# A GPS graph layer on one core: the last edges go into the table beside the first sort, and ScalarE makes the first 0/1 matrices

## The chip, the core and the metric

The kernel runs on one core of a Trainium2 chip. The time is that of one execution on the device, in microseconds (us). The engines are named as in the profile: PE is TensorE (PEld is its loading of weights), DVE is VectorE, ACT is ScalarE, POOL is GpSimd and SP is SyncE, which here issues DMA transfers. A transfer whose addresses come from a list of indices (a gather, or a scatter that adds) is issued by POOL.

## The reference, cut to what matters

One layer of a graph network over N = 6250 nodes with D = 256 features and E = 200 000 edges. Edge e goes from node `dst[e]` (whose row is read) to node `src[e]` (to which it is added). `src` is uniformly random. `dst` is skewed to low numbers, and the edges come sorted by `dst`.

```python
xn  = layernorm(x)
# 1. gated mean over edges
neigh = xn[dst]
w     = sigmoid(relu(neigh @ W1 + b1) @ W2 + b2)         # one gate an edge
num   = segment_sum(neigh * w, src, N); den = segment_sum(w, src, N)
gnn   = where(den > 0, num / max(den, 1e-12), 0)
# 2. a linear attention of 8 heads of 32 over all nodes
k, v  = head_ln(xn, klw, klb), head_ln(xn, vlw, vlb)     # d / (std + eps), std of n - 1
mix   = xn_heads @ (k^T v / N) + xn
x     = x + gnn + mix
# 3. six experts of three layers, the two best of each node mixed
f     = layernorm(x)
p     = softmax(relu(f @ rw1 + rb1) @ rw2 + rb2); top 2, softmax over these
out   = x + sum_top2 gate_e * (relu(relu(f @ ew1 + eb1) @ ew2 + eb2) @ ew3 + eb3)
```

The gate depends on the neighbour alone, so `w` and `neigh * w` are one row a node, and the edge part is a sum of such rows into segments. All is computed from the inputs on the chip, the order of the edges by `src` too.

## The kernel before

**The edges.** For each node the kernel makes a row of 258 numbers (neigh * w, w, 1), split into three bf16 terms whose sum carries the float32 value, and stores it in `y_rows`. The edges are cut by position. The first 65 536 (piece b, "hot") have neighbours in the first six node tiles of 128 and are handled by counting matrices, without gathers. The next 65 536 (piece a) and 65 536 (piece c) are "cold": their rows are gathered. The last 3392 are the "few", 27 tiles of at most 128.

**The sorts.** A cold piece is sorted by `src` with a bitonic network on DVE, 128 partitions by 512. Steps along a row are pairs of min and max (`first` and `step`, L263, L278, L279). When partitions have to be compared, `turned` (L308, L309) transposes the whole tile with four PE transposes and one ACT copy for each 512 columns, and back later. The first sort orders piece a alone. The second (`sort cb`) orders c and b side by side, 1024 wide, in 307 DVE instructions and 14 turns; its tiles are `k_cb` and `t_cb`. The sorted keys go to `list_a`, `list_c` and `list_b` in memory. Where each node tile's edges start in a list comes from `counts` (L361): one ACT `Sign` over the 128x512 sources with a sum, for each of the 48 borders between tiles, for a and for c; and 24 of them for b.

**The cold passes** (class `Cold`, L840 to L913). A pass takes a block of two node tiles (256 nodes). SP reads the start (a value load) and loads a window of 12 x 128 list entries for each tile and piece (`cold_load`, L790, L791). `decode` transposes the window on PE (L815), copies it on ACT (L817), and takes the two indices apart on DVE (`dsts` L824, `srcs` L826, `loc` L865). A step then handles 128 edges: POOL gathers 128 rows of `y_rows` (L877, tile `gt`), DVE makes a 128x128 0/1 matrix that says which edge goes to which node (L885, tile `hot`), and PE multiplies the matrix with the three terms (L902, tile `pu`). `make` runs ten steps ahead of the matmuls (AHEAD), with 20 buffers of `gt` and 16 of `hot`. The passes are six blocks of a (144 steps), the same six blocks of c (144), then the other blocks with both pieces (888): 1176 steps. When the first window of c is to be loaded, the rest of the second sort is written out first (`piece_sorted`). `decode` of the next pass is called at the 12th step of a pass.

**The few edges.** `few_equals` (L488 to L505) finds on DVE which of 128 edges share a target and to which row of `table` each writes. `few_edges` gathers 128 rows (L516, POOL), adds up those of one target with three matmuls (L532), copies the sums on ACT (L536, tile `sm`) and adds them into `table` with a scatter from POOL (L537). All scatters write the same table, so each waits for the one before to land. `table` is set to zero by SP beforehand (L445), and is read in the main part.

**The other work of the front.** `deviations` (L459 on) and two lines of `node_rows` (L551 to L606) make the normalized nodes and `y_rows`. `head_squares` (L659 to L686) and `heads` (L702 to L742) make the 32x32 head matrices. `expert_loads` (L959) loads the experts' weights through SP; the router's weights are loaded from ACT's queue (L943).

**The order.** The queues of PE, DVE, ACT, POOL and SP are written out in advance by a planner. Each of the jobs above is a `Line`, a generator that yields after each piece of work how many nanoseconds of DVE time it took and how long its next piece should wait. `run(lines, until)` takes the first line in the list that is due and whose `before` lines are closed, and moves a planned clock on. The first stage runs sort a, the nodes and the counts of a to their end. Then the cold steps of a start, and in the loop

```python
        while line_c.open:
            cold_edges.step()
            clock[0] += 200.0
            due += 2200.0
            run(beside, due)
```

one step alternates with 2200 ns of planned other work, until the few edges are done; a second loop goes on at 1300 ns a step until all jobs of the front are closed. Each engine works through its queue strictly in that order.

**The main part** then goes over the groups of four node tiles: `node_terms` (first matmul L1100), the hot edges by counting (L1047 to L1084), the cold steps of the blocks, and the router and six experts (L1203 to L1267; L1215, L1228 and L1245 are their three layers on PE), with the cold steps placed between the experts' matmuls.

Of the kernel before, what the change touches and what calls it, by code (L numbers as in the profile page):

```python
# [49 lines left out]
def kernel(  # L50
# [229 lines left out]

    def took(n):
        return 2 * (TT0 + 1.05 * n)

    def rows_sorted(k, name, width):

        h = 1
        while h < ROW:
            g = h  # L290
            while g:
                o = sp_small.tile([P, width], FP, name=f"k_{name}", bufs=2)
                if g == h:
                    first(k, o, h, last=2 * h == ROW)
                else:
                    step(k, o, g)
                k, g = o, g // 2
                yield took(width // 2), 0
            h *= 2
        return k  # L300

# [10 lines left out]
    def merged(k, name, width, m):  # L312

        t = turned(k, f"t_{name}", width)
        yield 0, TURN
        g = h = 1 << (m - 1)
        while g:
            o = sp_small.tile([P, width], FP, name=f"t_{name}", bufs=2)
            if g == h:
                first(t, o, h, last=2 * h == P)  # L320
            else:
                step(t, o, g)
            t, g = o, g // 2
            yield took(width // 2), 0
        k = turned(t, f"k_{name}", width)
        yield 0, TURN
        g = ROW // 2
        while g:
            o = sp_small.tile([P, width], FP, name=f"k_{name}", bufs=2)
            step(k, o, g)  # L330
            k, g = o, g // 2
            yield took(width // 2), 0
        return k


    TT0 = 150.0
    TURN = 2300.0


    pad = sp_small.tile([P, max(p.cap for p in pieces)], FP, name="pad")  # L340
# [11 lines left out]
            nc.sync.dma_start(lists[p.name][: p.n].rearrange("(p t) -> p t", p=P), k[:, i * ROW : (i + 1) * ROW])  # L352
            nc.sync.dma_start(lists[p.name][p.n :].rearrange("(p t) -> p t", p=P), pad[:, : p.cap])

    def counts(i):


        p = pieces[i]
        junk = sp_small.tile([P, p.row], BF, name=f"junk_{p.name}")
        for b in range(SB - 1 if p is hot else 0, NTHR, SB if p is hot else 1):  # L360
            nc.scalar.activation(  # L361
                junk, raw[p.name][0], AF.Sign, bias=thr[:, b : b + 1], accum_out=cnts[:, i, b : b + 1]
            )
            yield 0, 60 + 1.1 * p.row

    starts = const.tile([P, len(pieces), NTILE], I32, name="starts")
    nc.vector.memset(starts, 0)
# [140 lines left out]
    def few_edges():  # L508

        got = {}  # L510

        def gather(i):
            if i < NFEW:
                r = min(P, E - FEW - i * P)
                gt = gp.tile([P, TERMS, W], BF, name="gt")
                nc.gpsimd.indirect_dma_start(  # L516
                    out=gt[:r].rearrange("p k w -> p (k w)"),
                    out_offset=None,
                    in_=y_rows,
                    in_offset=bass.IndirectOffsetOnAxis(ap=few[1][:r, i : i + 1], axis=0),  # L520
                )
                got[i] = r, gt

        gather(0)
        gather(1)
        for i in range(NFEW):
            gather(i + 2)
            yield 0, 4500
            r, gt = got.pop(i)
            ps = p_t.tile([P, GT * P], FP, name="pT")  # L530
            for k in range(TERMS):
                nc.tensor.matmul(  # L532
                    ps[:r, :W], few_eq[:r, i, :r], gt[:r, k], start=(k == 0), stop=(k == TERMS - 1)
                )
            sm = nw.tile([P, W], FP, name="sm", bufs=3)
            nc.scalar.copy(sm[:r], ps[:r, :W])  # L536
            nc.gpsimd.indirect_dma_start(  # L537
                out=table,
                out_offset=bass.IndirectOffsetOnAxis(ap=few_row[:r, i : i + 1], axis=0),
                in_=sm[:r],  # L540
                in_offset=None,
                compute_op=ALU.add,
            )
# [76 lines left out]
    def run(lines, until=None):  # L620
# [16 lines left out]
        if until is not None:  # L637
            clock[0] = max(clock[0], until)


    worst = const.tile([P, 3], FP, name="worst")
    most = const.tile([P, 1], I32, name="most")
# [47 lines left out]
    def heads():  # L690
# [3 lines left out]
        for g, t0, nt, rows, r in groups:  # L694
            while g not in hsqs:
                yield 0, 1000
            xt, hsq = xts.pop(g), hsqs.pop(g)
            for j0 in range(0, nt, 2):
                k = min(2, nt - j0)
                for j in range(k):  # L700
                    for c in range(CB):
                        nc.tensor.matmul(  # L702
                            dv[:r, (j * CB + c) * P : (j * CB + c + 1) * P], xt[:, j0 + j, c, :r], centre,
                            start=True, stop=True,
                        )
                yield 0, 1800
                z = zs[j0 // 2]
                nc.vector.tensor_tensor(
                    z[:r, : k * CB, :P].rearrange("p b (h c) -> p b h c", c=HC),
                    dv[:r, : k * CB * P].rearrange("p (b h c) -> p b h c", h=HB4, c=HC),  # L710
                    hsq[:r, j0 * CB : (j0 + k) * CB, :, None].to_broadcast(
                        [r, k * CB, HB4, HC]
                    ),
                    op=ALU.mult,
                )
                for j in range(k):
                    for c in range(CB):
                        zc = z[:r, j * CB + c, :]
                        t = t0 + j0 + j
                        nc.tensor.matmul(  # L720
                            kv_ps[c][:, : P + 1], zc[:, :P], zc, start=(t == 0), stop=(t == NTILE - 1)
                        )
                yield 700, 0
# [38 lines left out]
    line_d = Line(deviations())  # L762
    lines_y = [Line(node_rows(i), before=[line_d]) for i in range(2)]
    line_t = Line(few_equals())
    line_c = Line(few_edges())
    line_u = [Line(counts(i)) for i in range(3)]
    line_a, line_b = Line(sort(pieces[:1])), Line(sort(pieces[1:]))
    line_q = Line(head_squares(), before=lines_y + [line_a])
    line_h = Line(heads(), before=lines_y + [line_t, line_a])
    line_l = Line(other_loads())  # L770
    line_e = Line(equal_keys(), before=[line_u[2], line_b, line_h])
    with tc.manual_schedule(engines=ORDERED):
        clock[0] = 6000.0
        line_d.due = 12000.0
        line_l.due = 16000.0
        line_u[1].before = line_u[2].before = lines_y
        line_t.before = [line_l]
        line_u[0].due = 9000.0
        first_lines = [line_u[0], line_l, line_d] + lines_y + [line_a, line_t]
        while any(a.open for a in first_lines):  # L780
            run(first_lines + [line_q, line_h, line_u[1], line_u[2], line_b], clock[0] + 1000.0)
        starts_of(0)


# [32 lines left out]
        nc.scalar.copy(keys.bitcast(FP), pT[:, :n])  # L817
        return keys, n

    def cold_window(wt):  # L820

        keys, n = window_keys(wt, "a")
        dsts = wn.tile([P, SB * NCOLD], I32, name="dsts")[:, :n]
        nc.vector.tensor_scalar(dsts, keys, (1 << LOW) - 1, None, op0=ALU.bitwise_and)  # L824
        srcs = wn.tile([P, SB * NCOLD], I32, name="srcs")[:, :n]
# [9 lines left out]
    for i, (blk, ps) in enumerate(passes):  # L835
        first_step.append(len(steps_c))
        for half in range(min(SB, NTILE - blk * SB)):
            n = sum(p.cap for p in ps)
            todo = range(half * n, (half + 1) * n)
            steps_c += [(i, half, j, j == todo[0], j == todo[-1]) for j in todo]  # L840

    class Cold:


        def __init__(self, sorted_to):
            self.made, self.done, self.loaded, self.sorted_to = 0, 0, 0, sorted_to
            self.wt, self.keys, self.gts, self.hot = {}, {}, {}, {}
            self.sums, self.parts = {}, {}
            self.load(0)
            self.load(1)  # L850
# [1 line left out]
        def load(self, i):  # L852

            while self.loaded <= min(i, len(passes) - 1):
# [3 lines left out]
                self.wt[self.loaded] = cold_load(blk, ps)  # L858
                self.loaded += 1

        def decode(self, i):
            self.load(i)
            dsts, srcs = cold_window(self.wt.pop(i))
            loc = wn.tile([P, SB * NCOLD], FP, name="loc")[:, : srcs.shape[1]]
            nc.vector.tensor_scalar(loc, srcs, float(-passes[i][0] * BN), None, op0=ALU.add)  # L865
            self.keys[i] = dsts, loc

        def make(self):
            i, half, j, _, _ = steps_c[self.made]
            at = self.made - first_step[i]  # L870
            if at == 2 and i + 1 < len(passes):
                self.load(i + 1)
            if at == 12 and i + 1 < len(passes):
                self.decode(i + 1)
            dsts, loc = self.keys[i]
            gt = gp.tile([P, TERMS, W], BF, name="gt")
# [5 lines left out]
            )  # L882
            self.gts[self.made] = gt
            hot1 = hp1.tile([P, P], BF, name="hot1")
            nc.vector.tensor_scalar(  # L885
                hot1, count[:, half * P : (half + 1) * P], loc[:, j : j + 1], None, op0=ALU.is_equal
            )
            self.hot[self.made] = hot1
            self.made += 1

# [34 lines left out]
    known = [cold[0]]  # L925
    with tc.manual_schedule(engines=ORDERED):
        cold_edges = Cold(lambda p: p is cold[0] or piece_sorted(p))
        beside = [line_c, line_u[1], line_q, line_h, line_u[2], line_b, line_e]
        run(beside[1:], clock[0] + 9000.0)
        cold_edges.decode(0)  # L930
        run(beside[1:], clock[0] + 2000.0)
        due = clock[0]
        while line_c.open:
            cold_edges.step()
            clock[0] += 200.0
            due += 2200.0
            run(beside, due)
    n_work.__exit__(None, None, None)

# [43 lines left out]


    line_w = Line(expert_loads())
    beside = [line_w, line_u[1], line_q, line_h, line_u[2], line_b, line_e]
    with tc.manual_schedule(engines=ORDERED):
        load(0)
        while any(a.open for a in beside):
            cold_edges.step()  # L990
            clock[0] += 200.0
            due += 1300.0
            run(beside, due)
        piece_sorted(cold[1])
    h_work.__exit__(None, None, None)
# [500 lines left out]
```

## Time and profile before

| | |
|---|---|
| time, median of 6 runs | 2354.19 us (2344.83 to 2363.0) |
| the profiled execution | 2363.96 us, of which the span of the trace is 2362.0 |
| mean granted TensorE clock over the span | 0.878 |
| PE busy | 1830.8 us (78%), 9541 matmuls; weight loads 1192.0 (50%) |
| DVE busy | 1259.3 us (53%), 5000 instructions |
| POOL busy | 1212.6 us (51%), 1243 instructions |
| ACT busy | 574.0 us (24%), 1199 instructions |

Durations below are those of the one profiled execution. "Issue" as the end of an idle time means that the engine waited for nothing that the profile shows; a name behind an arrow is the work that ended the wait. A weight load (PEld) runs beside the matmuls. A row of the view by stretches gives the stretch and its length, the busy time of PE, PEld, DVE, ACT and POOL with the number of instructions in brackets, the mean granted clock, the share of time that the 16 DMA engines were busy, and GB/s. In the groups a row has the line, engine and operation, the tiles written and read, the number, then the busy time and the mean of one in ns, then the idle time ahead of them and what ended most of it. A row of the waits has who waited for whom, the sum, the number and the longest, in us. In the chain, a row has the time, the length, and the work.

### The profile page before, as it was taken

What the parts mean: (1) busy time and instruction counts of PE and PEld (TensorE: products, weight loads), DVE (VectorE), ACT (ScalarE), POOL (GpSimd) and SP (SyncE); (2) the same over time, 40 slices, a digit from 0 to 9 for tenths busy, and PEclk for the clock granted to TensorE, in tenths of its full rate; (3) what the DMA queues carried; (4) which work ended last, traced back from release to release, by engine and by line L of the source; (5) the groups of instructions that cost most, each with busy time, mean ns of one, the idle gap of its engine ahead of it and who ended that gap; (6) DMA issues with size and microseconds to landing.
All of it is one profiled execution on the core that took longest, in us unless ns stands there. A gap on an engine that the chain in (4) does not pass through costs nothing.

```text
span 2362.0 us, 30158 instructions
## 1 busy us (share of the span) xinstructions
PE 1830.8 (78%) x9541; PEld 1192.0 (50%) x9541; DVE 1259.3 (53%) x5000; ACT 574.0 (24%) x1199; POOL 1212.6 (51%) x1243
## 2 busy tenths in 40 slices
PE   1571598543366898999889898998989889899997
PEld 0341377332243555655556555565655556556555
DVE  8699675664256553545435454454455535554321
ACT  6772542100001211212111121211212112122332
POOL 0000487874656566666666666566666656661000
PEclk9675599666687898999999999999999989999999
DMA  8650366564544455455555555555555555451000
GB/s 240 186 194 16 104 169 141 136 206 129 155 123 132 141 141 167 134 141 165 142 163 141 144 153 136 157 142 148 151 141 164 143 160 139 135 162 49 15 9 13
DMA packets 163584, 320.54 MB, mean 136 GB/s; under 512 B 31353, under 2 KB 104298, under 8 KB 163418
## 3 DMA queue, kind: packets, MB, share of 16 engines
q0 software_dynamic: 80800, 241.85, 37.9%
q1 hardware_dynamic: 77262, 76.15, 10.4%
q10 hardware_dynamic: 5356, 0.55, 0.3%
q8 instruction: 77, 1.26, 0.2%
q14 instruction: 89, 0.73, 0.1%
HBM read 285.06 MB, written 33.39 MB: 135 GB/s over the span
## 4 chain that ended last, share of the span: by engine, by line
PE 64%; DVE 6%; another core or an unknown queue 5%; issue 5%; DMA 2%; ACT 1%; POOL 1%; SPq 0%; DVEq 0%; POOLq 0%; ACTq 0%
PE px L1228 22%; PE pu L902 16%; PE px L1245 10%; PE ph L1075 5%; PE ph L1056 4%; PE px L1215 2%; PE ph L1100 1%; DMA gt<-y_rows,dsts 1%; DVE fr L1049 1%; PE px L1135 1%; DVE to L1047 1%; DVE hot L885 1%; PE turn L308 1%; DVE k_cb L278 1%
## 5 line engine op out<-in xcount | busy, mean ns | idle before, releaser
L877 POOL DMA_INDIRECT gt<-y_rows,dsts x1176 | 1132.8, 963 | 910.9 <-DVE srcs L826 263.7
L902 PE MATMUL pu<-gt,hot 128*128 128x258 bf16 x3528 | 604.1, 288 | 43.9 <-DMA gt<-y_rows,dsts 17.5
L902 PEld LDWEIGHTS <-hot 128*128 128x128 bf16 x3528 | 357.0, 103 | 415.8 <-issue 330.9
L1237 ACT ACTIVATE h<-px,eb_t 128x512 f32<-128x512 f32 (+1 forms) x312 | 206.3, 663 | 494.8 <-PE px L1228 203.1
L1228 PE MATMUL px<-fT,ew_t 128*128 128x512 f32 (+1 forms) x624 | 314.2, 599 | 1.6 <-issue 1.6
L1245 PE MATMUL px<-ew_t,h 128*128 128x256 f32 (+1 forms) x1176 | 303.2, 385 | 6.6 <-issue 5.3
L1228 PE MATMUL px<-h,ew_t 128*128 128x512 f32 (+1 forms) x624 | 300.6, 577 | 0.3 <-ACT fT L1129 0.2
L885 DVE TENSOR_SCALAR hot<-count,loc 128x128 bf16<-128x128 bf16 x1176 | 272.0, 273 | 31.9 <-remote 18.0
L1049 DVE TENSOR_SCALAR fr<-count,rdl 128x128 bf16<-128x128 bf16 x884 | 228.3, 274 | 108.9 <-PE pu L902 50.3
L1056 PE MATMUL ph<-to,fr 128*128 128x256 bf16 x884 | 189.9, 285 | 114.6 <-issue 59.0
L1254 DVE SCALAR_TENSOR_TENSOR acc<-px,gate,acc 128x256 f32<-128x256 f32 (+1 forms) x294 | 128.6, 478 | 247.3 <-PE px L1245 117.5
L1245 PEld LDWEIGHTS px<-ew_t,h 128*128 128x128 f32 (+1 forms) x1176 | 206.6, 192 | 38.5 <-issue 14.8
L1047 DVE TENSOR_SCALAR to<-count,hloc 128x256 bf16<-128x256 bf16 x612 | 184.6, 304 | 35.6 <-PE ph L1056 24.1
L1056 PEld LDWEIGHTS <-fr 128*128 128x128 bf16 x884 | 87.8, 100 | 147.8 <-issue 62.5
L1075 PE MATMUL ph<-yh,cn 128*128 128x258 bf16 x882 | 136.8, 280 | 31.0 <-issue 18.7
L1058 ACT CAST cn<-ph 128x256 bf16<-128x256 f32 x150 | 54.4, 374 | 355.9 <-PE ph L1056 210.3
L1075 PEld LDWEIGHTS <-cn 128*128 128x128 bf16 x882 | 87.6, 100 | 58.5 <-issue 43.5
L1228 PEld LDWEIGHTS px<-h,ew_t 128*128 128x128 f32 x624 | 97.0, 192 | 36.7 <-issue 31.9
L1228 PEld LDWEIGHTS px<-fT,ew_t 128*128 128x128 f32 x624 | 101.7, 201 | 24.9 <-issue 17.3
L817 ACT COPY keys<-pT 128x25 f32<-128x25 f32 (+2 forms) x56 | 10.5, 187 | 311.9 <-PE pu L902 94.6
L560 PE MATMUL turn<-ident,xs 128*128 128x128 f32 (+1 forms) x98 | 27.8, 407 | 74.5 <-ACT xs L551 68.1
L1103 DVE TENSOR_TENSOR u<-ph,u 128x256 f32<-128x256 f32 (+1 forms) x49 | 20.7, 423 | 108.0 <-PE ph L1100 38.4
(228 smaller groups left out, 1764.4 us busy)
## 6 DMA issues: line engine op xcount, KB each, us to landing
gt<-y_rows,dsts POOLq DMA_INDIRECT x1176
xs<-in_x_dram SPq DMA_DIRECT2D x24, 512.0 KB
y_rows<-ys SPq DMA_DIRECT2D x10, 774.0 KB
table<-zero SPq DMA_DIRECT2D x50, 129.0 KB
tb<-table SPq DMA_DIRECT2D x49, 129.0 KB
xnT_d<-xnT SPq DMA_DIRECT2D x12, 512.0 KB
xt<-xnT_d SPq DMA_DIRECT2D x12, 512.0 KB
u<-in_x_dram SPq DMA_DIRECT2D x12, 512.0 KB
```

The lines of the kernel that those rows point to most:

```text
L877: nc.gpsimd.indirect_dma_start(out=gt.rearrange("p k w -> p (k w)"), out_offset=None, in_=y_rows, in_offset=bass.IndirectOffsetOnAxis(ap=d ...
L885: nc.vector.tensor_scalar(hot1, count[:, half * P : (half + 1) * P], loc[:, j : j + 1], None, op0=ALU.is_equal)
L902: nc.tensor.matmul(self.pu, hot1, gt[:, k], start=(start and k == 0), stop=(stop and k == TERMS - 1))
L1047: nc.vector.tensor_scalar(made[j1], count, loc[:, j1 : j1 + 1], None, op0=ALU.is_equal)
L1049: nc.vector.tensor_scalar(fr, count[:, :P], rdl[:, d1, j1 : j1 + 1], None, op0=ALU.is_equal)
L1056: nc.tensor.matmul(pa, matrices[i], made[j], start=(j == j0), stop=(j == j1 - 1))
L1058: nc.scalar.copy(cn[:, d], pa)
L1075: nc.tensor.matmul(pu[:, :W], cn[:, d, s * P : (s + 1) * P], yh[:, d, k], start=(d == 0 and k == 0), stop=(d == HOT - 1 and k == TERMS - 1),)
L1228: nc.tensor.matmul(ph[:, :rows], w[:, e, c, f * P : (f + 1) * P], ins[:, c, :rows], start=(c == 0), stop=(c == CB - 1),)
L1237: nc.scalar.activation(h[:, f, :rows], ph[:, :rows], AF.Relu, bias=bc)
L1245: nc.tensor.matmul(po[:r, j - j0], h2[:, c, j * P : j * P + r], ew_t[2][:, e, c, :], start=(c == 0), stop=(c == CB - 1),)
L1254: nc.vector.scalar_tensor_tensor(acc[:r, j, :], po[:r, j - j0], gate[:r, j, e : e + 1], acc[:r, j, :], op0=ALU.mult, op1=ALU.add)
```

## The change

1. **The few edges** start as soon as `node_rows`, `few_equals` and the zeroing of the table are closed, in the first stage beside sort a, ahead of all other lines in the list, at 2400 ns of planned wait a tile instead of 4500. The gathers are issued four ahead instead of two, and `sm` has four buffers instead of three. `few_equals` waits for no line now and is first due at 62 us of the planned clock.
2. **The 0/1 matrices of the first six passes** (144 steps; ON_ACT) are made by two ACT instructions, |loc - count| and then relu(1 - that), instead of one DVE comparison. `loc` has its sign turned for it.
3. **Turn and decode apart.** The window of the next pass is transposed and copied at step 8 of a pass (`turn`), and taken apart on DVE at step 13 (`decode`); both were at step 12.
4. **Counts.** 28 of the 48 counts of piece a stay early, and 20 are made when the rows are done. Those of c and b follow after sort a and at the end of the list. The scrap tile `junk` is one name with two buffers.
5. **Head squares** may start when the rows and the counts of a are done, and no longer wait for sort a.
6. **The planner's figures** are set anew: the price of a sort step and of a turn, the planned times per cold step (2200 to 4100, 1300 to 1500) and the order of the lines.

The core of the diff:

```diff
-    def took(n):
-        return 2 * (TT0 + 1.05 * n)
+    def took(n, apart=False):
+        return 4 * (TT0 + 0.52 * n) if apart else 2 * (TT0 + 1.05 * n)
...
-    TT0 = 150.0
-    TURN = 2300.0
+    TT0 = 120.0
+    TURN = 2600.0
...
-    def counts(i):
+    def counts(i, part=slice(None)):
...
-            yield 0, 60 + 1.1 * p.row
+            yield 0, 900
...
-        gather(0)
-        gather(1)
+        for i in range(4):
+            gather(i)
+        yield 0, 2400
         for i in range(NFEW):
-            gather(i + 2)
-            yield 0, 4500
+            gather(i + 4)
+            yield 0, 2400
...
-            sm = nw.tile([P, W], FP, name="sm", bufs=3)
+            sm = nw.tile([P, W], FP, name="sm", bufs=4)
...
-    line_c = Line(few_edges())
-    line_u = [Line(counts(i)) for i in range(3)]
+    line_l = Line(other_loads())
+    line_c = Line(few_edges(), before=lines_y + [line_t, line_l])
+    line_u0 = Line(counts(0, slice(0, EARLY)))
+    line_u = [Line(counts(0, slice(EARLY, None)), before=lines_y)] + [Line(counts(i)) for i in (1, 2)]
...
-    line_q = Line(head_squares(), before=lines_y + [line_a])
+    line_q = Line(head_squares(), before=lines_y + [line_u[0]])
...
-            run(first_lines + [line_q, line_h, line_u[1], line_u[2], line_b], clock[0] + 1000.0)
+            run([line_c] + first_lines + [line_q, line_b], clock[0] + 1000.0)
...
-    def cold_window(wt):
-
-        keys, n = window_keys(wt, "a")
+    def cold_window(keys, n):
+
...
+    ON_ACT = LEAD
+
...
+            if i < ON_ACT:
+                nc.vector.tensor_scalar(loc, srcs, -1.0, first, op0=ALU.mult, op1=ALU.add)
+            else:
+                nc.vector.tensor_scalar(loc, srcs, -first, None, op0=ALU.add)
...
-            if at == 12 and i + 1 < len(passes):
+            if at == 8 and i + 1 < len(passes):
+                self.turn(i + 1)
+            if at == 13 and i + 1 < len(passes):
                 self.decode(i + 1)
...
+            if i < ON_ACT:
+
+                away = hp1.tile([P, P], BF, name="away", bufs=2)
+                nc.scalar.activation(away, count[:, half * P : (half + 1) * P], AF.Abs, bias=loc[:, j : j + 1])
+                nc.scalar.activation(hot1, away, AF.Relu, bias=ones[:, 0:1], scale=-1.0)
+            else:
+                nc.vector.tensor_scalar(
+                    hot1, count[:, half * P : (half + 1) * P], loc[:, j : j + 1], None, op0=ALU.is_equal
+                )
...
-        beside = [line_c, line_u[1], line_q, line_h, line_u[2], line_b, line_e]
-        run(beside[1:], clock[0] + 9000.0)
+        beside = [line_t, line_c, line_u[1], line_q, line_h, line_b, line_u[2], line_e]
+        run(beside, clock[0] + 9000.0)
+        cold_edges.turn(0)
+        run(beside, clock[0] + 3000.0)
         cold_edges.decode(0)
-        run(beside[1:], clock[0] + 2000.0)
+        run(beside, clock[0] + 2000.0)
         due = clock[0]
         while line_c.open:
             cold_edges.step()
-            clock[0] += 200.0
-            due += 2200.0
+            clock[0] += 30.0 if cold_edges.made < first_step[ON_ACT] else 270.0
+            due += 4100.0
             run(beside, due)
```

## The prediction

> **What bounds the kernel now.** I read the time by stage first, from busy times in stretches whose ends I took from the timeline: first gather of the cold edges at 264 us, end of the second sort at 572, first expert matmuls about 780, last gather about 2130.
>
> ```profile
> 0.00:264.00 264.00, 103.65 (x361) 63.14 (x362) 216.50 (x642) 158.74 (x351) 1.62 (x12) 0.70 0.51 150
> 264.00:545.00 281.00, 180.12 (x1146) 143.03 (x1145) 172.63 (x418) 70.36 (x177) 218.97 (x188) 0.76 0.62 159
> 545.00:610.00 65.00, 25.82 (x148) 18.52 (x148) 31.88 (x87) 3.83 (x9) 30.95 (x32) 0.64 0.47 138
> 800.00:2130.00 1330.00, 1193.97 (x6284) 756.84 (x6285) 663.52 (x3075) 259.09 (x498) 844.85 (x890) 0.95 0.53 148
> 2130.00:2362.00 232.00, 214.83 (x910) 136.95 (x909) 77.83 (x296) 65.59 (x122) 7.68 (x9) 0.97 0.07 19
> ```
>
> After the two stretch numbers come PE, PEld, DVE, ACT and POOL. From 800 us on PE is full (90%, then 93%). What can be won in front of that is time in which PE waits. Up to 264 DVE is the full engine (216.5 of 264) and POOL does nothing. From 264 to 545 no engine looks full, so I took POOL's groups there:
>
> ```profile
> L877 POOL DMA_INDIRECT gt<-y_rows,dsts x133 | 141.3, 1063 | 305.3 <-DVE srcs L826 262.0 <-issue 27.9 <-remote 4.8
> L537 POOL DMA_INDIRECT table<-sm,few_row x27 | 49.0, 1816 | 10.3 <-issue 6.1 <-ACT sm L536 2.1 <-ACT sq L672 1.2
> L516 POOL DMA_INDIRECT gt<-y_rows,dst_c x27 | 29.0, 1073 | 8.2 <-issue 4.3 <-PE pu L902 1.8 <-PE pT L532 0.9
> ```
>
> Each of the 187 is followed by 0.3 us that no wait explains ("issue"): 219 + 187 x 0.3 = 275 of 281 us. POOL is full there, and 78 + 54 x 0.3 = 94 us of it is the few edges. Everything else stands in one written order with it, the turns of the second sort (c and b, 1024 wide) too. The chain shows what its end releases:
>
> ```profile
> 569.43 2.79 DMA gt<-y_rows,dsts
> 572.73 3.79 DMA list_c<-pad
> 576.65 0.38 SPq L791
> 577.08 0.49 SPq L790
> 578.02 1.51 DMA wt_a<-list_c
> 579.93 7.62 PE pu L902 x45
> ```
>
> No edge of piece c can be gathered before list_c is stored, and no node's sum is complete before piece c's passes. So **572 us is the gate**: what comes after it (1790 us) is the same work in both kernels and starts 34 us behind it (first L1100 at 606). In the changed program's order 156 steps of cold edges stand ahead of that line, 154 before. I forecast by how far the gate moves. DVE's waits from 264 to 573:
>
> ```profile
> DVE t_cb L263 <- ACT t_cb L309: 36.4, 7, 13.8
> DVE k_cb L278 <- ACT k_cb L309: 11.6, 6, 2.8
> DVE z L708 <- PE dv L702: 10.2, 5, 4.8
> DVE dsts L824 <- ACT junk_b L361: 9.9, 1, 9.9
> DVE hot L885 <- remote: 9.7, 4, 3.3
> ```
>
> Most is DVE waiting for a turn that PE and ACT reach late.
>
> **The change, part by part. First stage.**
> *Counts.* Of 48 counts of piece a on ACT (0.72 + 0.19, spaced 0.85 us) 20 move behind the rows. 19 stand between 41 and 76 us now, about nine of them ahead of the first w, for which DVE waits 10.3 us. Nine times 0.85: -8 us for the rows, and for DVE.
> *Few equals, earlier.* 8 x (0.59 + 0.38 + 0.59) = 12 us of DVE move from 133-215 to the rows' stretch. DVE is 86% busy there and serves the sort in both places: 0. If the rows wait for it, up to 12.
> *Decode of the first pass.* DVE waits 7.1 us for ACT's keys at 263; now the turn is issued earlier and sort steps stand between: -7.
> *More of the second sort ahead.* In the order, 85 of its 307 instructions stand before the first decode, 65 before: 20 x 0.65 = +13 here, and as much less later.
> *Few edges.* 27 gathers, 27 x 3 matmuls, 27 ACT copies (0.375) and 27 scatters move into the first sort; POOL has 1.6 us of work there, so its 94 us are covered. But every scatter waits until the one before has landed in the table, and all engines' later work queues behind. The chain prices it:
>
> ```profile
> 447.73 3.94 DMA table<-sm,few_row
> 451.88 3.21 DMA gt<-y_rows,dsts
> ```
>
> That is 3.94 + 0.3 = 4.2 us a step where scatters follow each other. 22 of them now stand before the first cold gather on POOL. The last rows are stored at 185.6 us now, 8 earlier then; gather, landing, matmul and copy add 6: 184 + 22 x 4.2 = 276. On DVE's side it is 264 - 8 - 7 + 13 + some 7 for turns of sort a that stand behind matmuls waiting on gathers and behind 20 counts = 269. POOL is later: **first cold gather 276, +12**. Bounds: 264 (scatters as close as POOL allows, 1.8 + 1.1 + 0.6 = 3.5) to 290 (5 us each).
>
> **Second stage, 276 us to the gate.** Three engines, each by itself:
> - DVE: 222 sort instructions left, 111 steps x 1.29 = 143; 25 z (17), hsq (7), kv and decodes (7) = 31; 14 turns, of which an undisturbed one takes 3.4 (last t_cb step over at 557.0, k_cb starts 560.4) = 48. Sum 222; with the 31 inside the turns 191. What it loses: 127 matrices (31.6 busy) and their waits (14.7).
> - POOL: 122 gathers up to the flush of the sort x 1.36 + 5 scatters x 2.1 = 177, then 28 of sort alone (16 steps, 2 turns) = 205. The 27 few cost 94 there before.
> - ACT: 122 matrices, each two dependent ACTIVATEs of 128x128. No such row exists. Below it stands w, 128x4, at 0.26, above it the 128x512 rows at 0.66; between them 128x256 at 0.497 (L593). On the line through the first and last of these, 0.38; two make 0.72 with their overlap. 122 x 0.72 = 88, 62 counts x 0.85 = 53, 28 copies 14, squares 12, rest 7 = 174, plus 28 = 202. At the lower row 122 x 0.52: 178; at the upper 122 x 1.33: 276.
>
> The matrices are made ahead, but now a turn's copy queues behind them on ACT, and behind that DVE. The router loads on ACT (L943) still wait for the last scatter; the t_cb copy lost 18.9 us behind them, 0 to 19 again. I take the longest, 222, and add 20 for the three standing in each other's way: 276 + 242 = **518, -54**. Ends: 276 + 191 = 467 and 276 + 276 + 10 = 562.
>
> A rule of the Trainium skill speaks against this part (ScalarE: Activation LUTs, Rules for kernel authors: relu and adds belong on VectorE, not ScalarE). The rows agree on the engine time, 0.275 us for one on DVE against 0.72; taken as the whole price, 88 - 32 = 56 us would be given back and the gate would stand near 572 again. I hold that POOL's order, not DVE's work, kept the gate, and ACT had 70 of 281 us to do.
>
> *Expert weights on SP.* 18 x 256 KB now come before list_c; four came after it. SP had issued list_c by 573.7: 0. Head squares two groups earlier: the 13.6 us wait of L670 for xt goes, inside the 20.
>
> **Main stage.** The turn of a pass's keys stands 4 steps earlier, the decode 1 later. DVE waits at L824 from 842 on in 14 stretches of over 2 us, 93.6 us together, in which PE was busy 72.0: at most 21.6 to win. The lists are loaded about 45 us ahead (1294.4 against 1340.7), so no new wait. I take -8; ends 0 and -21.
>
> **Sum.** -54 - 8 = -62 on the profiled execution (2363.96, span 2362.0 + 2 around it): 2302. The median of the runs shown is 9.8 lower, 2354.19: **2292 us**.
>
> **Rivals.**
> 1. *ACT takes POOL's place.* Matrices at 0.66 an operation; gate near 562, -10, with -4 in the main stage: 2340. For it: ACT's queue is strictly in order. Against: 128x256 already takes only 0.497.
> 2. *The other side: turns stuck in the queue.* If each of the 14 turns costs 11 us (2 of 14 now cost 13.8 and 12.5) because ACT's copy stands behind matrices and PE's behind matmuls waiting on gathers, 276 + 143 + 31 + 154 = 604: +32, 2386. It decides from (572 - 276 - 174) / 14 = 8.7 us a turn. Against: the mean idle at turns is now 51/13 = 3.9 with POOL full.
> 3. *The few edges eat the first stage.* Scatters at 6 us (their spacing now): first gather 316, of which some 20 is made good by the sort going on: gate 545, 2322.
> 4. *All three engines overlap well:* gate about 480 and 15 in the main stage: 2247.
>
> **How the numbers follow.** Forecast 0.52, rival 1 0.13, rival 2 0.13, rival 3 0.12, rival 4 0.10. Half a per cent, 12 us, is about what a measurement of this kernel can tell. Faster: the forecast, rivals 3 and 4, and half of 1 (0.07): 0.81; same, most of the rest of 1: 0.05; slower: rival 2 and what is left of 1: 0.14. The range leaves out rival 2 and part of 4: 2252 (gate -90) to 2345. The forecast's own range is 2265 to 2325.
>
> **What would show it.** Right: list_c issued near 518; POOL between 276 and then near 90% with only 5 scatters; two ACT rows of 0.35 to 0.45 us; scatters 4.2 apart before 276; first kv matmul 30 to 36 us behind list_c; the stretch from there on as long as now within 20 us; L824's waits in it near none. Wrong: a t_cb wait of DVE over 9 us on average; ACT above 90% busy in the second stage; first cold gather after 290; or a main stage longer than now by more than 15 us, for which I see no cause.

## The result and the profile after

The changed kernel takes 2357.74 us (median of 42 runs) against 2351.51 us before (84 runs). The ratio is 1.0024, with a 95% interval of 1.0012 to 1.0035. That is a quarter of a per cent slower, inside the half per cent that I had called no change. I had forecast 2292 us with a range from 2252 to 2345, so the measured time lies outside it. The profiled execution took 2363.35 us, with a span of 2361.6.

Four of the stretches as before, in the changed kernel (stretch and length, then busy time of PE, PEld, DVE, ACT and POOL with the number of instructions, granted clock, DMA share, GB/s):

```profile
0.00:264.00 264.00, 116.32 (x404) 69.67 (x404) 219.65 (x648) 139.31 (x297) 44.85 (x43) 0.68 0.60 167
264.00:545.00 281.00, 167.96 (x1093) 134.74 (x1093) 151.57 (x289) 170.66 (x474) 169.99 (x157) 0.77 0.54 148
800.00:2130.00 1330.00, 1196.73 (x6298) 760.45 (x6297) 665.19 (x3083) 259.29 (x503) 847.43 (x893) 0.95 0.54 149
2130.00:2361.00 231.00, 215.75 (x907) 137.19 (x905) 76.88 (x292) 63.79 (x118) 6.51 (x7) 0.97 0.07 18
```

The work did move as the diff says. POOL is busy for 45 us in the first stretch (1.6 before), and ACT for 171 us in the second (70 before). In the second stretch POOL went down from 219 to 170 us and DVE from 173 to 152. Nobody is full there any more, and yet the stage ends at the same time. The stores of the two sorted lists, in the line on SP's queue (duration min/median/max in ns, first and last start in us), changed kernel:

```profile
L352 SPq DMA_DIRECT2D list_a<-k_a x1: 362/362/362, 259.3 to 259.3; - x1
L352 SPq DMA_DIRECT2D list_c<-k_cb x1: 383/383/383, 572.1 to 572.1; - x1
```

The same two in the kernel before:

```profile
L352 SPq DMA_DIRECT2D list_a<-k_a x1: 363/363/363, 245.9 to 245.9; - x1
L352 SPq DMA_DIRECT2D list_c<-k_cb x1: 362/362/362, 572.3 to 572.3; - x1
```

The first sort ends 13.4 us later, the gate is where it was. The first gather of the cold edges is at 308.4 us, against 264.2 before and 276 forecast. DVE's waits from the end of the first sort to 364 us show what stood still (who waited for whom, sum, number, longest, in us); then PE's from 195 to 364:

```profile
DVE z L711 <- PE dv L705: 36.3, 6, 17.9
DVE hsq L688 <- issue: 18.5, 1, 18.5
```

```profile
PE pT L533 <- DMA gt<-y_rows,dst_c: 42.5, 9, 13.2
PE pu L923 <- DMA gt<-y_rows,dsts: 20.3, 1, 20.3
```

PE waits for the gathers of the few edges, and then 20 us in one piece for the first cold gather. Behind PE's waiting matmuls stands the `dv` that DVE's `z` needs, and behind that `z` the sort. The longest of these waits, in PE's and DVE's rows (start, length, [idle before <- what ended it]; the `dv` between them starts at 315.95):

```profile
311.68 0.80 PE L923 MATMUL pu<-gt,hot 128*128 128x258 bf16 x3 [20.33 <-DMA gt<-y_rows,dsts]
317.04 0.69 DVE L711 TENSOR_TENSOR z<-dv,hsq 128x512 f32<-128x512 f32 x1 [17.89 <-PE dv L705]
```

DVE had spent 65 us on instructions of the second sort by 320 us before, and 55 in the changed kernel; by 400 us 94 and 79. POOL's own record shows the pace, in the same view:

```profile
206.45 1.61 POOL L538 DMA_INDIRECT table<-sm,few_row  x1 [1.70 <-DMA table<-sm,few_row]
208.36 1.17 POOL L516 DMA_INDIRECT gt<-y_rows,dst_c  x1 [0.30 <-issue]
211.13 1.59 POOL L538 DMA_INDIRECT table<-sm,few_row  x1 [1.60 <-ACT sm L537]
213.02 1.02 POOL L516 DMA_INDIRECT gt<-y_rows,dst_c  x1 [0.30 <-issue]
215.69 1.58 POOL L538 DMA_INDIRECT table<-sm,few_row  x1 [1.66 <-issue]
```

A tile of few edges takes 4.6 to 4.7 us where nothing disturbs it, and 4.93 on average (22 scatters from 201.80 to 305.31). The planner reckons with 2.4 here; in the kernel before it had 4.5.

### The profile page after: what moved, and what is told of

The parts are those of the page before. It is cut to its first block, busy times and chain, and to the rows that moved or that the text cites. A ratio compares the mean times of both kernels' runs of the same rounds, so it can differ in the third digit from the quotient of the medians.

```text
span 2361.6 us, 30298 instructions
## 1 busy us (share of the span) xinstructions
PE 1841.1 (78%) x9541; PEld 1194.9 (51%) x9541; DVE 1238.4 (52%) x4856; ACT 668.5 (28%) x1487; POOL 1206.4 (51%) x1243
## 4 chain that ended last, share of the span: by engine, by line
PE 61%; another core or an unknown queue 8%; DVE 7%; ACT 5%; issue 4%; SPq 0%; ACTq 0%; DMA 0%; DVEq 0%
PE px L1251 21%; PE pu L923 15%; PE px L1268 10%; PE ph L1079 4%; PE ph L1098 4%; PE px L1238 2%; DVE to L1070 1%; DVE fr L1072 1%; PE px L1158 1%; DVE k_cb L278 1%; DVE k_cb L279 1%; ACT junk L361 1%; PE ph L1123 1%; ACT hot L904 1%
## 5 line engine op out<-in xcount | busy, mean ns | idle before, releaser
L1251 PE MATMUL px<-fT,ew_t 128*128 128x512 f32 (+1 forms) x624 | 313.4, 599 | 0.0
L1251 PE MATMUL px<-h,ew_t 128*128 128x512 f32 (+1 forms) x624 | 299.1, 574 | 1.5 <-issue 0.8
L906 DVE TENSOR_SCALAR hot<-count,loc 128x128 bf16<-128x128 bf16 x1032 | 239.6, 276 | 38.0 <-PE pu L923 18.5
L516 POOL DMA_INDIRECT gt<-y_rows,dst_c x27 | 30.0, 1113 | 200.2 <-DVE k_a L279 192.3
L1251 PEld LDWEIGHTS px<-fT,ew_t 128*128 128x128 f32 x624 | 101.7, 201 | 24.5 <-issue 16.8
L1251 PEld LDWEIGHTS px<-h,ew_t 128*128 128x128 f32 x624 | 96.9, 192 | 32.6 <-issue 26.8
L1108 DVE TENSOR_TENSOR cs<-ph,cs 128x258 f32<-128x258 f32 x49 | 20.9, 427 | 147.5 <-PE pu L923 75.1
```

What stands on the lines that cost most here:

```text
L906: nc.vector.tensor_scalar(hot1, count[:, half * P : (half + 1) * P], loc[:, j : j + 1], None, op0=ALU.is_equal)
L1251: nc.tensor.matmul(ph[:, :rows], w[:, e, c, f * P : (f + 1) * P], ins[:, c, :rows], start=(c == 0), stop=(c == CB - 1),)
```

## The experiments

My theory after this reading was that the chain of scatters, twice as slow as the planner's figure, holds up the queues of all engines from 195 us on. The rivals were that ACT's matrices hold up the turns of the second sort, that POOL still bounds the second stage, and that this stage has a length of its own.

All kernels in one table. "Ahead" is the number of few-edge scatters that stand before the first cold gather in POOL's order. Times are us from the profiled execution, the ratio is to the kernel before, with its interval. The last four ran on a chip where the kernel before took 2379.2 us instead of some 2355, so for these the ratio is what compares; in proportion, an estimate, 1789.6 us to the end would be 1808 there. Each row of times is one execution, while the ratio is that of the medians.

| kernel | ahead | first cold gather | list_c | between | list_c to end | ratio |
|---|---|---|---|---|---|---|
| before | 0 | 264.2 | 572.3 | 308.1 | 1789.7 | 1 |
| changed | 22 | 308.4 | 572.1 | 263.7 | 1789.5 | 1.0024 (1.0012 to 1.0035) |
| changed, four tables | 22 | 276.4 | 529.4 | 253.0 | none | none |
| changed, 4700 ns | 12 | 270.4 | 529.0 | 258.6 | 1789.6 | 0.9847 (0.9821 to 0.9874) |
| changed, matrices on DVE | 22 | 315.4 | 583.3 | 267.9 | 1795.4 | 1.0097 (1.0067 to 1.0126) |
| before, matrices on ACT | 0 | 266.0 | 572.1 | 306.1 | 1794.1 | 0.9995 (0.9974 to 1.0016) |
| 4700 ns, matrices on DVE | 12 | 273.0 | 539.7 | 266.7 | 1797.9 | 0.9844 (0.9775 to 0.9913) |
| 4700 ns, turn and decode at 12 | 12 | 271.2 | 526.8 | 255.6 | 1798.3 | 0.9844 (0.9781 to 0.9906) |
| before, few edges early, 4700 ns | 14 | 276.5 | 538.7 | 262.2 | 1791.4 | 0.9875 (0.9813 to 0.9937) |
| changed, 7000 ns | 8 | 269.1 | 540.3 | 271.2 | 1811.3 | 0.9995 (0.996 to 1.003) |
| before, few edges early, 2400 ns | 27 | 333.8 | 603.9 | 270.1 | 1823.4 | 1.0134 (1.0086 to 1.0181) |
| changed, 3600 ns | 17 | 288.0 | 539.4 | 251.4 | 1811.2 | 0.9885 (0.9842 to 0.9929) |
| 4700 ns, heads late | 12 | 268.4 | 490.2 | 221.8 | 1852.3 | 0.9853 (0.9806 to 0.99) |
| 4700 ns, few_equals later | 12 | 263.2 | 520.6 | 257.4 | 1813.2 | 0.982 (0.9768 to 0.9871) |

### Scatters to four tables in turn

```diff
+    tables = [table] + [dram.tile([TROWS, W], FP, name=f"table{i}") for i in range(1, 4)]
...
-                out=table,
+                out=tables[i % 4],
```

> The changed kernel, with the 27 scatters of the few edges going in turn to four tables, so that a scatter need not wait for the one ahead of it; the sums of three of the four tables are left out of the result. Theory (the chain of the few edges, 4.63 us a tile in the trace where the planner reckoned with 2.4, holds up the queues of PE, ACT and DVE from 195 to 344 us): a tile then takes what POOL needs, 1.6 + 1.0 + 2 x 0.3 = 3.2 us, the first cold gather comes near 275 instead of 308, list_c is stored near 540 instead of 572, time 30 us or so below the changed kernel, ratio to before 0.985 to 0.992. Rival A (the matrices on ACT hold up the turns of the second sort): list_c within 10 us of 572, ratio 0.998 to 1.005. Rival B (the second stage has a bound of its own, from the first cold gather on): list_c as early as the first gather, near 540, as by the theory; told apart by the stage's own length, which is 264 us now: 264 again by rival B, shorter or longer by the theory as the stalls at 300 to 363 go.

The kernel counts at its end how many edges it has summed, and goes through all edges again in a slow loop if any are missing. With three of the four tables left out of the sum it did so, and its span of 25 742.7 us tells nothing; only the front, up to the stores of the lists, is read here. POOL's record, in the same view as above:

```profile
206.77 1.75 POOL L539 DMA_INDIRECT table<-sm,few_row  x1 [0.31 <-issue]
208.82 1.14 POOL L517 DMA_INDIRECT gt<-y_rows,dst_c  x1 [0.30 <-issue]
210.27 1.58 POOL L539 DMA_INDIRECT table<-sm,few_row  x1 [0.30 <-issue]
```

```profile
L353 SPq DMA_DIRECT2D list_a<-k_a x1: 363/363/363, 249.5 to 249.5; - x1
L353 SPq DMA_DIRECT2D list_c<-k_cb x1: 382/382/382, 529.4 to 529.4; - x1
```

Without the wait for the landing most tiles take 3.2 to 3.5 us. The first cold gather comes 32.0 us earlier and list_c 42.7 us earlier, and the first sort too ends 9.8 us earlier. Nothing else was changed, the ACT matrices least of all, so the wait of a scatter for the landing of the one before is the cause of these 43 us. Rival A is refuted. What is left is close to rival B: 253 us from the first cold gather to list_c, where it was 264.

### The few edges at the pace that they take: 4700 and 3600 and 7000 ns

```diff
-        yield 0, 2400
+        yield 0, 4700
         for i in range(NFEW):
             gather(i + 4)
-            yield 0, 2400
+            yield 0, 4700
```

> The changed kernel, with the planner told 4700 ns for a tile of few edges instead of 2400, which is what a tile took (4.63 us). 12 scatters then stand ahead of the first cold gather instead of 22, and the rest between the cold steps. Theory (queues held up because the chain was reckoned too short): DVE's waits for dv and hsq between 260 and 363 us (58 us now) fall below 20, first cold gather near 265, list_c near 540, ratio to before 0.983 to 0.992. Rival A (ACT's matrices): list_c within 10 us of 572, ratio 0.998 to 1.005. Rival C (POOL is the bound of the second stage, and every scatter put back there costs it): first gather early, but list_c still after 560.

It took 2321.51 us, 0.9847 of the kernel before, and so faster than both kernels, with the planner's two figures alone. The list of piece c:

```profile
L352 SPq DMA_DIRECT2D list_c<-k_cb x1: 383/383/383, 529.0 to 529.0; - x1
```

The waits that answer to those above, DVE's from 248 to 364 us and PE's from 195 to 364:

```profile
DVE z L711 <- PE dv L705: 35.1, 12, 8.9
DVE hsq L688 <- ACT hsq L686: 4.3, 2, 2.6
```

```profile
PE pu L923 <- DMA gt<-y_rows,dsts: 3.3, 1, 3.3
PE pT L533 <- DMA gt<-y_rows,dst_c: 2.5, 1, 2.5
```

PE's waits for gathers, 62.8 us, are 5.8. The gate is where it was in the experiment before (529.4), by another means. Here the wait for the landing is still there, but nothing is queued behind it too early. DVE's waits for `dv` and `hsq` did not fall below 20 as I expected: for `dv` there are twice as many of half the length, with nearly the same sum. So these waits alone do not make up the 43 us of the gate. Up to list_c DVE works 392 us in both kernels, and what falls is its idle time, from 180 to 137 us: by 12 us from 195 us to the end of the first sort (the changed kernel's waits there, 11.6 us, are for turns of that sort), by 18 from there to 364, and by 14 behind that. Rival C is refuted: 15 scatters back beside the cold steps did not bring the gate back.

> The changed kernel with 3600 ns a tile, between 2400 (22 scatters ahead of the first cold gather, 2357.7 us) and 4700 (12, 2321.5). 17 scatters stand ahead. Theory: first cold gather at 202 + 17 x 4.6 = 281 to 286, second stage 253 to 271, list_c 535 to 555, time 2330 to 2345. Rival (a tile costs only when the queues' order is wrong by more than some amount): first gather below 275 and time within 6 us of 2321.5.

Between the two, as the theory has it, is the first gather, at 288.0. It is 2 us later than I expected, and the second stage, 251.4, is shorter than I expected and the shortest with the heads in it; list_c at 539.4 lies where I had it. The ratio, 0.9885, is below that of the changed kernel, and in proportion the time is 2328 us, a little under the 2330 to 2345 that I expected; but its interval overlaps that of 4700 ns, so these two times are not told apart.

> The changed kernel with 7000 ns a tile of few edges: 8 scatters ahead of the first cold gather, 19 beside the cold steps (12 and 15 with 4700, 22 and 5 with 2400). Theory (with 4700 the stalls are gone, and what is left is DVE, with POOL next): first cold gather near 264, list_c 520 to 540, time within 10 us of 2321.5. Rival (still held up by the chain in the first stage at 4700): list_c before 515, time below 2310. Other rival (POOL bounds, each scatter put back costs its 3 us): list_c after 541.

This one missed. The gate is at 540.3, but the time is that of the kernel before. The rival that POOL bounds the stage had put list_c after 541, and the stage, 271.2 us, is the longest of all changed orders: with 19 scatters put back, this rival is not refuted here. 1811.3 us lie between list_c and the end, 21.7 more than with 4700, and 13 to 20 more than in the three other kernels on the same chip (1791.4 to 1798.3). The count of gathers offers a reason: 119 cold gathers had been issued when list_c was stored, against 136 with 4700, 139 in the changed kernel and 142 before. The loop around the few edges lets 4100 planned ns pass for each cold step, the one behind it 1500, and with 7000 ns a tile the first loop lasts longer. 17 gathers at 1.25 us each are 21 us. Of the 21.7 us, 17.6 lie ahead of the first matmul of the experts' first layer (L1251), which starts 233.8 us behind list_c here and 216.2 with 4700. So the trace fits this reason, but no run of its own tests it.

### The matrices, each way

```diff
-    ON_ACT = LEAD
+    ON_ACT = 0
```

> The changed kernel, with the 0/1 matrices of all passes made by DVE again, all else left. Theory (few edges' chain): the 122 matrices put 32 us of work back on DVE, which waits far longer than that in the stage, so list_c within 12 us of 572 and the ratio to before 0.998 to 1.008. Rival A (the matrices on ACT delay the turns and head squares, and with them DVE): list_c before 550, ratio 0.985 to 0.992.

> The kernel before, with only the matrices of the first six passes moved to ACT (two ACT instructions each), no other part of the change. Theory (in the kernel before POOL's order is what bounds 264 to 545): list_c within 10 us of 572, ratio 0.995 to 1.003. Rival A (ACT's matrices hold up the turns): list_c after 585, ratio 1.006 to 1.015. By my forecast's reckoning of DVE's losses (32 us of matrices and 15 us of waits for them) the other way: list_c near 550, ratio near 0.99.

> The changed kernel with 4700 ns a tile of few edges (2321.5 us, list_c stored at 529), and the 0/1 matrices of all passes made by DVE. On the kernel before, moving them to ACT alone gave nothing (0.9995, list_c 572.1); on the changed one, moving them back cost 23 us (2380.6 against 2357.7). Theory (the matrices cost only where DVE bounds the second stage, and with the few edges out of the way it nearly does): list_c 15 to 40 us later than 529, time 2338 to 2362. Rival (they never matter by themselves): list_c within 8 us of 529, time 2315 to 2330.

Moved to ACT in the kernel before, the matrices gain nothing that shows: list_c 572.1, ratio 0.9995. Moved back to DVE, they cost 11.2 us of the gate in the changed kernel (583.3 against 572.1) and 10.7 with 4700 ns (539.7 against 529.0). In the last case the times are not told apart (0.9844 against 0.9847). On the changed kernel the ratio, 1.0097, is just above what my theory allowed (1.008); with 4700 ns list_c came earlier than it had, and neither it nor its rival fits both figures. So rival A, that ACT's work holds up the sort, has the sign wrong, and my forecast, which took 31.6 us of busy time and 14.7 of waits off DVE, has the size wrong by a factor of four. The pair itself cost nearly what I had worked out (0.38 for one, 0.72 for both): 0.79 us busy and 0.73 from one pair to the next (line, engine, operation, tiles, number | busy us, mean ns | idle before), changed kernel, from 292 to 572 us:

```profile
L904 ACT ACTIVATE hot<-away,ones 128x128 bf16<-128x128 bf16 x128 | 51.4, 401 | 4.1
L903 ACT ACTIVATE away<-count,loc 128x128 bf16<-128x128 bf16 x128 | 49.7, 389 | 0.0
```

### The few edges alone, on the kernel before

The core of the edit; with it go the four gathers ahead, the fourth buffer of `sm`, the earlier `few_equals` and the pace of a tile (4700 or 2400 ns).

```diff
-    line_c = Line(few_edges())
+    line_c = Line(few_edges(), before=lines_y + [line_t, line_l])
...
-            run(first_lines + [line_q, line_h, line_u[1], line_u[2], line_b], clock[0] + 1000.0)
+            run([line_c] + first_lines + [line_q, line_h, line_u[1], line_u[2], line_b], clock[0] + 1000.0)
```

> The kernel before, with only the few edges moved beside the first sort (four gathers ahead, four sums' buffers, few_equals earlier) at 4700 ns a tile; matrices stay on DVE, and counts, turn and planner figures stay as before. Theory (POOL's order was the bound of 264 to 545 in the kernel before, and the few edges were 94 us of it): list_c 20 to 45 us earlier than 572, time 2312 to 2336. Rival (without the matrices moved, DVE and POOL change places as the bound): list_c after 560, time 2345 or more.

> The kernel before, with only the few edges moved beside the first sort, at 2400 ns a tile as the change has it (with 4700 ns the same move gave 2328). All 27 scatters then stand ahead of the first cold gather. Theory (a tile takes 4.6 us, and the second stage takes its 253 to 271 us from the first cold gather on, as in every run so far): first cold gather at 202 + 27 x 4.6 = 327, list_c 580 to 596, time 2368 to 2392. Rival (in the kernel before the early scatters find more slack, since the matrices and the counts stand otherwise): time at or below 2340.

The same move is worth 0.9875 at 4700 ns and 1.0134 at 2400. With 2400 all 27 scatters stand ahead of the first cold gather, which comes at 333.8, and the gate at 603.9, both later than I expected (327, and 596 at most) on a chip that is 1% slower. That is the clearest pair: one number of the planner decides between 1.25% faster and 1.3% slower.

### Turn and decode

```diff
-            if at == 8 and i + 1 < len(passes):
+            if at == 12 and i + 1 < len(passes):
                 self.turn(i + 1)
-            if at == 13 and i + 1 < len(passes):
+            if at == 12 and i + 1 < len(passes):
                 self.decode(i + 1)
```

> The changed kernel with 4700 ns a tile, and turn and decode of the next pass both back at step 12. From list_c to the end of the span it is 1789.7 us before, 1789.5 changed, 1789.6 with 4700 ns, though DVE's waits for the keys after 700 us fall from 99.6 to 22 us. Theory (these waits cost nothing, PE is full there): time within 8 us of 2321.5, and 1785 to 1795 from list_c to the end, with the waits back at 60 us or more. Rival (my forecast's): 8 us or more longer from list_c on.

DVE's waits for the keys after 700 us, in the kernel before, in the changed one, and then with 4700 ns and turn and decode back at 12 (with 4700 ns alone they sum to 22 us, as in the changed kernel):

```profile
DVE dsts L824 <- ACT keys L817: 76.7, 13, 12.3
DVE dsts L824 <- issue: 22.9, 6, 10.2
```

```profile
DVE dsts L827 <- ACT keys L821: 15.6, 4, 6.4
DVE dsts L827 <- issue: 5.5, 1, 5.5
```

```profile
DVE dsts L827 <- ACT keys L821: 103.9, 17, 12.2
```

The waits come back in full, and the time does not move (2321.31 against 2321.51). In the profiled execution the stretch behind list_c is 8.7 us longer, which is what the rival says and outside what the theory allowed (1785 to 1795), but the medians do not show it. The intervals of the two ratios (0.9781 to 0.9906, 0.9821 to 0.9874) leave room for 8 us. So the 80 us of waits are worth far less than their sum, and whether they are worth 0 or 8 us is not shown.

### What sets the second stage: the heads late

```diff
-    line_h = Line(heads(), before=lines_y + [line_t, line_a])
+    line_h = Line(heads(), before=lines_y + [line_t, line_a, line_b])
```

> The changed kernel with 4700 ns a tile, and the heads (dv on PE, z on DVE, kv on PE, 25 pieces) held until the second sort has ended. What sets the 253 to 271 us from the first cold gather to list_c? Theory 1 (DVE's waits for dv, 47 us with 4700 ns, and the z themselves, 17): at most 225 us, list_c before 500; the node terms need kv, so the main part then starts later behind list_c, more than 1789.6 from it to the end. Theory 2 (the turns of the sort, each with PE and ACT in the queue's order, and the cold steps): still 245 us or more.

The stage falls to 221.8 us and the list is stored at 490.2:

```profile
L352 SPq DMA_DIRECT2D list_c<-k_cb x1: 383/383/383, 490.2 to 490.2; - x1
```

In every other changed order it was 251 to 271 us. So the heads in DVE's queue, with their waits for PE, make up some 37 us of it (258.6 with 4700 ns), of which 32 are less work on DVE (128 us busy against 160). Part of what they leave is taken by waits for the turns, 59 us now against 26 with 4700 ns (from the first cold gather to list_c):

```profile
DVE k_cb L278 <- ACT k_cb L309: 36.3, 5, 17.7
DVE t_cb L263 <- ACT t_cb L309: 22.5, 5, 10.3
```

The time gains nothing (0.9853), since the heads then stand ahead of the main part, which needs them: 1852.3 us from list_c to the end, where 1808 would be in proportion.

### few_equals later

```diff
-        line_t.due = 62000.0
+        line_t.due = 120000.0
```

> The changed kernel with 4700 ns a tile, and few_equals (12 us of DVE) first due at 120 us of the planned clock instead of 62. My forecast had the last rows stored 8 us earlier than before (185.4) for the counts moved; they were 2 to 3 us later (187.4, with 4700 ns 188.5). Theory (few_equals' DVE time, put ahead of the rows, took what the counts gave): last store of the rows at 175 to 181, first few gather at 182 to 188 instead of 195.7, time within 8 us of 2321.5. Rival (the rows have another bound): last store 186 to 190.

The last store of the rows is issued at 182.1 us, 6.4 earlier than with 4700 ns (188.5) and a microsecond outside what I expected; the first gather of the few edges is at 191.1 instead of 195.7, three outside. The first sort ends at 241.5, 6.8 earlier. The ratio, 0.982, is the lowest of all, but its interval overlaps that of 4700 ns alone.

## Why the prediction was wrong, point by point

- **What bounds it: right.** I took the store of list_c as the gate and all behind it as fixed. From that store to the end of the span it is 1789.7 us before, 1789.5 changed and 1789.6 with 4700 ns. What I left out is how many cold gathers have been issued by then, which the run with 7000 ns suggests counts too. Of the 66 us by which the time lies above the forecast, 32 are the first cold gather, 22 the second stage and 8 the main stage; the other 4 are the distance from the profiled execution to the median, 5.6 us here against the 9.8 that I took.
- **"First cold gather 276, +12": the step that failed.** It came at 308.4, outside my bounds of 264 to 290. Of the 32 us too many, the rows are 10: I had the last store 8 us earlier for the counts moved, and it was 2 later (187.4 against 185.4). "Few equals, earlier: 0" is most of that: the run with few_equals later gave 6.4 us back (I had named up to 12 us as its other end). What the other 4 are is open. 8 us are the way from that store to the first scatter: the first gather started at 194.5, 7 us behind the last store. I take this for the landing of the rows, which the profile does not name, and I had counted 6 us for the whole way. 14 us are the pace, 4.93 us a tile on average against my 4.2, which was the transfer's row and 0.3 behind it alone.
- **"On DVE's side 269": failed with it.** I gave 7 us to turns that stand behind matmuls waiting on gathers. The first sort alone ended 13.4 us later, and between 262 and 317 us DVE had waits of 13.8 and 17.9 us for `dv`. I wrote that all engines' later work queues behind a scatter, and then priced POOL's queue and these 7 us only. The four tables and the pace of 4700 ns, each by itself, give 43 us of the gate back.
- **Second stage, "222 and 20": too short.** It took 263.7 us from the first cold gather to list_c, against 242. DVE was busy for 155.5 us of it, less than the 143 and 31 I had for steps and the rest. The mis-sized term is the waiting: I had 48 us at the turns and 20 for the three engines standing in each other's way, and DVE was idle for 108 us (99 of 258.6 with 4700 ns). The heads alone are worth 37 us of the stage. (In ACT's sum, 28 copies at 0.587 us are 16 us and not 14, which decided nothing.)
- **Matrices.** The duration was right, the gain a quarter of what I took. A rule of the Trainium skill (ScalarE: Activation LUTs, Rules for kernel authors) puts relu and adds on VectorE. The rows agree with it on the engine time: a matrix takes 0.73 us on ScalarE and 0.275 on VectorE. Moving the matrices to ScalarE was still worth 11 us of the gate in two settings, and nothing in a third. The 56 us given back that I had worked out from the two durations do not show. That the queue in which the work stands decided, and not its duration, is my reading; no run tests it apart.
- **Main stage, "-8": 0.** The waits at the decode went from 99.6 us to 22, as the change means to, and the stretch from list_c to the end stayed the same in the profiled executions (1789.7 and 1789.5).
- **The rivals.** The third was the nearest: its mechanism, the few edges eating the first stage, is what happened, and its first gather at 316 was close to 308. It failed where it let the sort go on meanwhile and so made good 20 us; DVE stood still with the rest. (Its sum was off as well: 518 + 40 - 20 is 538, not 545.) The second had turns stuck, with the same in-order queues as its reason, but put the loss at the turns. DVE's waits for turns in that stage sum to 36.5 us there, 2.6 for each of the 14, far from the 8.7 from which it would have decided.

## What to carry to other kernels

A transfer that must wait for the landing of the one before it has a pace of its own (here 4.6 to 4.7 us a tile against 3.2 to 3.5 without the wait), and when several in-order queues are written out from one plan, the plan needs that pace. Too short a figure cost every engine here, since each queue met work that waits on the chain too early. Price a moved chain by the first waiting instruction on each queue and what stands behind it, and not only by the engine that issues it.

An engine that waits less, or does less, need not shorten the whole: two of the single edits here (the matrices on the kernel before, turn and decode) moved 32 us of busy time and 80 us of waits, and left the total where it was, as far as the runs can tell.

## What I had not expected of the hardware

The stretch behind the gate, some 1790 us with some 8000 matmuls, came out within 0.2 us in the profiled executions of three kernels and at 1791 to 1798 us in five others on chips of the same speed (1811.3 with 7000 ns), while the single runs of one kernel spread over 5 to 33 us. So the agreement within 0.2 us is partly luck. And one chip ran the kernel before in 2379.2 us, 1% longer than the 2351 to 2356 of the others.
